# New order lists for a hand-scheduled scan kernel, and the last step of a batch sent from its own buffers

## The chip, the cores and the metric

The kernel runs on one core of a Trainium2 chip. The metric is device time in microseconds, the median of the runs; the kernel before has a median of 1783.09 us over 3 runs (1782.42 to 1785.32). The core has five engines that work side by side and wait for each other through semaphores: PE (matrix multiplies), DVE (vector), ACT (scalar functions), POOL (GpSimd) and SP, which here only issues transfers. Each engine, and each queue of transfers, works strictly in the order in which its instructions were written.

## The reference

A map of 4 batches x 128 channels x 96 x 96 is normalised in 32 groups of channels, read in four directions (rows forward and backward, columns forward and backward), and each sequence of 9216 positions goes through the same small state-space block. The four results are fused by a 1x1 convolution and added to the input.

```python
t = _grouped1x1(x, in_proj_w, in_proj_b, G)
u, gate = (t[:, :HID], t[:, HID:])
u = jax.nn.silu(u)
u = lax.conv_general_dilated(u, dw_w, ..., feature_group_count=HID)
s = _conv1x1(u, ssm_in_w)
a = DMIN + (DMAX - DMIN) * jax.nn.sigmoid(_conv1x1(u, ssm_delta_w, ssm_delta_b))
...
hst = jnp.exp(prefix) * jnp.cumsum(bb * s * jnp.exp(-prefix), axis=-1)
u = u + _conv1x1(cc * hst + ssm_d[None, :, None] * s, ssm_out_w)
u = _grouped1x1(u * jax.nn.sigmoid(gate), mix_w, mix_b, G)
return _conv1x1(u, out_proj_w, out_proj_b)
```

## The kernel before, in words

**Tiling.** A batch is worked on in two phases, columns ("V") and then rows ("H"). A phase has 6 steps of 4 units, so a phase has 24 units, a batch 48, and the kernel 192 (`NPAIR`). A unit is a pair: 384 positions of the forward sequence and 384 of the backward one, treated together. In the second half of a phase the backward sequence passes the places that the forward one has passed before, so the in-projection and the gates of the first half are kept in DRAM and read again instead of being computed twice.

**Operations.** Each unit goes through about sixty named operations. Those that the text speaks of:

- `F0` to `F3`: in-projection on PE, four matmuls of 32 rows x 32 columns each, from the tile `x_in`; `SIL0` to `SIL3`: silu on ACT (L650), which empties the PSUM bank into the tile `sil`. `zero_ends` (L657) clears the first column at the start of a sequence.
- `C0`, `C1`, `L`: depthwise convolution of the first 128 channels on PE (tiles `band`, `less`), emptied by `UC` on ACT (L751). `T0` (ACT, L786) and `T1` to `T4` (DVE, L788): the five taps for the other 128 channels.
- `P0a` to `P1b`: projections to the scan's operands on PE (`u,main`), emptied by `TM`, `SC`, `CT` on ACT. `DEC` (L826) and `BS` (L829) on POOL prepare the scan, `SCAN0` and `SCAN1` on DVE (L846) run it for a whole step, `CH`, `ADD`, `CP` on POOL (L852, L856, L859) take its result on.
- `S` and `G`: output of the scan and gates on PE (L869, L875); `GAT` on DVE (L922); `W`: mix, output projection and fusion as one product on PE (`u,w_fin`).
- `YS0`, `YS1`: ACT copies the result of a unit's two sequences from PSUM into tiles `ys` (two buffers for sequence 0, one for sequence 1; L933, L935). `ACC0`, `ACC1` (L975): POOL adds them to `acc`, the sum of the whole map, which starts as the input. `send` (L939) writes finished parts of `acc` to the output, `load_next` (L949) fills them with the next batch's input for the next sums.

**What sets the order.** Everything from the first in-projection on is recorded under a manual schedule: the order in the code is the order on each engine. Units 0 to 7 run by the list `START` (L153), the last 6 and what is still open by `END` (L116), and in between one slot per unit by one of four lists in `PLAN` (L65) that are repeated: "front" where the in-projection runs, "gate" where gates are computed, "both" and "none". `LAGS` (L87) says how many slots behind the slot's own number an operation's unit lies, `BANKS` which of the 8 PSUM banks it asks for, `MOVES` in which order the slot's transfers are issued, all on SP. In the lists a star marks the same work on another engine (`DEC*` on DVE, `CP*` on ACT, `ACC0*` straight from PSUM on DVE).

**The opening.** Before the schedule starts, `load_x` (L394) loads batch 0 in pieces of 1 to 4 chunks of 384 columns and DVE runs one `bn_stats` (L398) on each chunk; the sums give the normalisation, which is folded into the weights `wn`, and with these the first in-projection can start. Weights (`small`, `fuse`, `main`) are loaded between the pieces.

**The batch change.** A part of `acc` is worked through three times by transfers: after its last sum `send` writes it out, after that transfer has landed `load_next` overwrites it with the next batch's input, and only after that may POOL add the next batch's first results to it. For the very last step of the kernel (L972) the sums go to the free tile `x_in` and out from there.

Of the kernel before, what the change touches and what calls it, by code (L numbers as in the profile page):

```python
# [47 lines left out]
P = 128  # L48
# [18 lines left out]
        T1 F1 F3 CP YS1 TM F2 F0 DEC P1b T2 P0b W01 AU0 SIL1 SIL3 SIL0 W00 SC BS T3 T4 SIL2 ZERO  # L67
        UND1 SCAN0 UND0 AU1 YS0 G00 C0 C1 S11 CT SS S00 ACC0 ACC1 S10 G01 SCAN1 S01 CH BN G10 E
        AFTER TH0 G11 L W10 W11 GAT0 TH1 UC P0a GAT1 ADD TH2 P1a T0 TH3
    """,  # L70
    "both": """
        YS1 T1 F2 F0 TM CP SCAN1 T2 F3 F1 C0 C1 SIL1 SIL0 P0b SIL2 T3 DEC SIL3 ZERO P1b L S11
        S10 T4 CT CH G10 SS G00 UC ADD TH2 W01 UND1 E AFTER W00 SC G01 ACC1 BN S01 YS0 ACC0 S00
        UND0 G11 AU1 TH0 GAT1 AU0 W10 W11 TH1 SCAN0 BS GAT0 P0a P1a T0 TH3
    """,
    "gate": """
        P0b YS1 CP AU1 P1b ACC1 T1 TM T2 AU0 UND1 C1 DEC CT C0 SC W00 L T3 SS T4 UND0 W01 BS S11
        E AFTER SCAN1 S10 G00 CH UC YS0 S00 G01 G11 TH0 BN S01 ACC0 G10 SCAN0 TH1 GAT1 W11 W10
        ADD P1a T0 P0a TH3 GAT0 TH2
    """,  # L80
    "none": """
        C0 T1 C1 TH1 P0b L W00 CP T2 P1b YS1 W01 TH0 TM ACC1 TH3 UND0 CH UC S01 E AFTER UND1 SC
        DEC T3 YS0 S00 G10 G11 AU0 S10 S11 T4 SCAN1 CT G01 BS BN G00 ADD SCAN0 GAT1 ACC0 AU1 TH2
        T0 P0a W10 SS W11 P1a GAT0
# [12 lines left out]
        "TB": 3, "CB": 7, "SS1": 6, "PA": 6, "W0b": 0, "W1b": 6, "Fb3": 7, "Gb0": 3, "Gb3": 4  # L97
    },
    "both": {
        "SS1": 6, "PB": 6, "W0b": 2, "Fb2": 7, "Fb3": 7, "Gb3": 4  # L100
    },
    "gate": {
        "SS0": 2, "SS1": 3, "PB": 3, "W0b": 1, "W1b": 3, "Fb1": 7, "Fb2": 7, "Fb3": 7, "Gb1": 2,
        "Gb3": 3
    },
    "none": {
        "SS0": 4, "SS1": 6, "PB": 6, "W1b": 7
# [9 lines left out]
    YS1:-14=3 C1:-6 TM:-7=7 CP*:-12 C0:-6=0 W00:-13 T1:-6=2 W01:-13=2 T2:-6 P0b:-7=0 P1b:-7=3  # L117
    UND1:-12 E:-6 UND0:-12=1 ACC1:-14 T3:-6 S10:-12=4 T4:-6 S00:-12 YS0:-13=0 SC:-7 DEC:-7
    S11:-12=5 S01:-12=0 GAT0:-12=2 T0:-5=5 W11:-13 ACC0:-13 T1:-5=2 W10:-13=0 CH:-11 BS:-7
    ACC1*:-13 ADD:-11 C0:-5=6 CT:-7=6 GAT1:-12=6 P0a:-6=7 C1:-5 CH:-10 UND0:-11=0 CP:-11 T2:-5=7  # L120
    P1a:-6=1 TM:-6=4 L:-5 W00:-12 CH:-9 T3:-5 P0b:-6=7 ADD:-9 W01:-12=5 S00:-11=6 UC:-5
    UND1:-11=4 DEC:-6 T4:-5=6 S01:-11=7 ACC0*:-12 S11:-11 T0:-4=5 GAT0:-11 S10:-11=4 SS:-8
    P0a:-5 P1a:-5=1 W11:-12=7 P1b:-6=4 W10:-12=7 TM:-5=1 T1:-4=3 P1b:-5=6 SC:-6 CT:-6=6 YS1:-12
    ADD:-10 T2:-4 P0b:-5=2 T3:-4=2 C0:-4 W00:-11=6 SC:-5=5 GAT1:-11=6 DEC:-5 BS:-6 T4:-4=6
# [22 lines left out]
    W11:-3=7 CP:-1 W10:-3=2 UND1:-1 GAT1:-2=2 W00:-2=6 S11:-1=3 ACC1*:-3 S01:-1 S00:-1=3 S10:-1  # L147
    YS1:-6 YS1:-4=0 W01:-2=5 YS0:-3=1 YS1:-3 W10:-2 W11:-2 GAT0:-1=2 W00:-1 ACC0*:-2 W01:-1=0
    YS1:-2=6 GAT1:-1=4 ACC1*:-2 YS0:-2=7 W11:-1=0 ACC0*:-1 W10:-1=0 YS1:-5=6 YS0:-1 ACC1*:-1
    YS1:-1=0  # L150
"""
TAIL = 6
START = """  # L153
# [1134 lines left out]
```

## Time and profile before

| | |
|---|---|
| median of 3 runs | 1783.09 us (1782.42 to 1785.32) |
| profiled execution | 1780.91 us, of which its span is 1779.2 us |
| mean granted PE clock | 0.991 |
| PE / DVE / ACT / POOL busy | 1751.6 / 1519.3 / 1484.4 / 1400.3 us |
| HBM read / written | 222.96 / 151.18 MB |

The profile is of one execution. "Busy" is the time in which an engine has at least one instruction under way. PE's instructions overlap (four matmuls on separate quarters of the array run at once, and each matmul is two records), so its pace is read from the distance of the starts, not from the length of one record. The name of a tile stands without its number in the profile (`u,main` are the projections, `u,w_fin` the result products, `sil,band` the convolution, `x_in,wn` the in-projection and, in L875, the gates).

### The profile page before, as it was taken

To read this page: it belongs to the slowest core of one execution; us is meant where nothing else is said; L and a number is where in the kernel's file an instruction comes from. 1 tells how busy PE (TensorE), PEld (TensorE's weight loads), DVE (VectorE), ACT (ScalarE), POOL (GpSimd) and SP (SyncE) were. 2 spreads that over 40 slices of the span, in tenths; PEclk is the share of its full clock that TensorE was granted. 3 is DMA by queue.
4 is the path that set the end of the run, shared out by engine and by line. 5 is a ranking of instruction groups with operands and counts; after the bars stand their busy time and mean duration, and the time that the engine had idled before them with its cause. 6 is when DMAs were issued, how large, how long until landed. Compare 5 with 4: busy or idle time off the path is not lost.

```text
span 1779.2 us, 54578 instructions
## 1 busy us (share of the span) xinstructions
PE 1751.6 (98%) x22584; PEld 641.0 (36%) x22584; DVE 1519.3 (85%) x1550; ACT 1484.4 (83%) x2571; POOL 1400.3 (79%) x1493
## 2 busy tenths in 40 slices
PE   6999999999999999999999999999999999999998
PEld 3333333333333333333333333333333333333333
DVE  4898988888788988988788888898888878888898
ACT  4888888888888888888887888888888888888875
POOL 4488888778778888788777888878778788887776
PEclk7999999999999999999999999999999999999999
DMA  6767676665987678564798657755588755655654
GB/s 211 193 217 241 186 224 179 200 218 165 296 261 240 207 207 241 181 203 166 217 288 263 229 188 226 222 178 196 165 268 264 249 197 185 207 162 187 227 179 158
DMA packets 183143, 377.69 MB, mean 212 GB/s; under 512 B 16752, under 2 KB 146928, under 8 KB 182896
## 3 DMA queue, kind: packets, MB, share of 16 engines
q1 hardware_dynamic: 182752, 374.16, 67.1%
q8 instruction: 178, 2.92, 0.7%
q14 instruction: 69, 0.57, 0.1%
q10 hardware_dynamic: 144, 0.04, 0.0%
HBM read 222.96 MB, written 151.18 MB: 210 GB/s over the span
## 4 chain that ended last, share of the span: by engine, by line
PE 90%; DMA 3%; ACT 3%; issue 1%; SPq 1%; DVE 1%; POOL 1%; POOLq 0%; ACTq 0%; DVEq 0%
PE psum L246 76%; PE psum L869 9%; PE psum L875 4%; DMA out<-acc 1%; ACT gate L881 1%; DMA acc<-in_xr 1%; DMA main<-in_main 1%; POOL acc L975 1%; ACT psum L865 0%; SPq L716 0%; SPq L396 0%; DVE u L769 0%; ACT u L751 0%; DVE u L922 0%; POOL t L852 0%
## 5 line engine op out<-in xcount | busy, mean ns | idle before, releaser
L788 DVE SCALAR_TENSOR_TENSOR psum<-sil,small,psum 128x768 f32<-128x768 f32 x576 | 588.3, 1021 | 52.3 <-ACT psum L786 33.8
L246 PE MATMUL psum<-u,w_fin 128*32 128x384 f32 x6144 | 580.4, 490 | 1.9 <-DVE u L769 0.6
L246 PE MATMUL psum<-u,main 128*32 128x384 f32 x6144 | 563.7, 489 | 2.1 <-ACT gate L881 0.8
L975 POOL TENSOR_TENSOR acc<-ys,acc 128x384 f32<-128x384 f32 x368 | 427.5, 1170 | 154.6 <-ACT ys L935 77.6
L922 DVE SCALAR_TENSOR_TENSOR u<-gate,psum 128x768 f32<-128x768 f32 x376 | 345.9, 950 | 98.1 <-PE psum L869 67.9
L246 PEld LDWEIGHTS psum<-u,main 128*32 128x32 f32 x6144 | 186.9, 110 | 327.6 <-issue 218.2
L246 PEld LDWEIGHTS psum<-u,w_fin 128*32 128x32 f32 x6144 | 175.4, 109 | 344.3 <-issue 234.8
L865 ACT COPY psum<-u 128x768 f32<-128x768 f32 x352 | 278.0, 801 | 24.7 <-DVE u L769 8.4
L246 PE MATMUL psum<-sil,band 128*32 128x384 f32 x3072 | 287.0, 488 | 4.5 <-ACT ys L935 2.5
L852 POOL TENSOR_TENSOR t<-t,t 64x384 f32<-64x384 f32 x192 | 235.0, 1225 | 65.4 <-DVE t L846 29.2
L869 PE MATMUL psum<-t,main 32*128 32x384 f32 x1536 | 258.1, 531 | 2.6 <-ACT psum L865 2.3
L856 POOL TENSOR_TENSOR t<-t,t 64x384 f32<-64x384 f32 x192 | 237.3, 1236 | 7.6
L881 ACT ACTIVATE gate<-psum,bnorm 128x384 f32<-128x384 f32 x384 | 211.5, 576 | 35.5 <-PE psum L869 14.9
L829 POOL TENSOR_TENSOR t<-t,tm 64x384 f32<-64x384 f32 x192 | 194.8, 1014 | 52.4 <-ACT t L812 35.0
L826 POOL TENSOR_SCALAR t<-tm 64x384 f32<-64x384 f32 x189 | 181.1, 958 | 66.6 <-issue 31.0
L650 ACT ACTIVATE sil<-psum,bnorm 128x385 f32<-128x385 f32 x384 | 200.1, 580 | 27.5 <-PE psum L246 26.6
L788 DVE SCALAR_TENSOR_TENSOR u<-sil,small,psum 128x768 f32<-128x768 f32 x192 | 194.6, 1013 | 18.6 <-DVE psum L788 0.5
L786 ACT ACTIVATE psum<-sil,small 128x768 f32<-128x768 f32 x192 | 173.8, 905 | 35.1 <-DVE u L922 27.4
L875 PE MATMUL psum<-x_in,wn 32*128 32x384 f32 x768 | 186.5, 516 | 0.2
L804 ACT ACTIVATE tm<-psum,small 128x384 f32<-128x384 f32 x192 | 112.4, 585 | 58.0 <-PE psum L246 55.9
L935 ACT COPY ys<-psum 128x384 f32<-128x384 f32 x281 | 134.5, 479 | 24.7 <-POOL acc L975 13.6
L246 PEld LDWEIGHTS psum<-sil,band 128*32 128x32 f32 x3072 | 97.4, 110 | 155.8 <-issue 104.3
(84 smaller groups left out, 1446.6 us busy)
## 6 DMA issues: line engine op xcount, KB each, us to landing
sil<-sil SPq DMA_DIRECT2D x128, 770.0 KB, 7.2
kept<-gate SPq DMA_DIRECT2D x80, 768.0 KB, 4.3
gate<-kept SPq DMA_DIRECT2D x76, 768.0 KB, 5.9
edge<-edge SPq DMA_DIRECT2D x96, 384.0 KB, 5.8
x_in<-in_xs SPq DMA_DIRECT2D x192, 96.2 KB, 3.7
edge<-sil SPq DMA_DIRECT2D x96, 192.5 KB, 3.5
out<-acc SPq DMA_DIRECT2D x44, 384.0 KB, 3.4
acc<-in_xr SPq DMA_DIRECT2D x38, 384.0 KB, 8.4
```

What stands on the lines that cost most here:

```text
L246: nc.tensor.matmul(o[r, : rhs.shape[-1]], lhsT, rhs, start=start, stop=stop, skip_group_check=True)
L650: nc.scalar.activation(sils[step][:, s, j, g, :], bank(frm)[:, : N + 1], AF.Silu, bias=bn[:, 1:2] if j else bn[:, 4 + g : 5 + g],)
L788: nc.vector.scalar_tensor_tensor(u_of(n)[:, :, 1, :] if k == K - 1 else part, src, w_tap[:, k : k + 1], part, ALU.mult, ALU.add,)
L829: nc.gpsimd.tensor_mul(scan_of(n)[0:64, pair_of(n)["p"], :], tbs[n][0:64, :], tms[n][0:64, :])
L852: nc.gpsimd.tensor_mul(ta[0:64, p, :], tbs[n][64:P, :], ta[64:P, p, :])
L856: nc.gpsimd.tensor_add(z, scans[n // R][0:64, pair_of(n)["p"], :], z)
L865: nc.scalar.copy(two(to), us[n][:, s])
L869: nc.tensor.matmul(bank(to)[:, :N], w_so[r, bass.ts(j, P)], tbs[n][r, :], start=not seeded(n), stop=True, skip_group_check=True)
L875: nc.tensor.matmul(bank(to)[:, :N], stats[pair_of(n)["b"]][0][r, s, :], x_in[s][r, q, off : off + N], start=True, stop=True)
L881: nc.scalar.activation(gates[n % 2][:, s, j, :], bank(frm)[:, :N], AF.Tanh, bias=bn[:, 2 + j : 3 + j], scale=0.5,)
L922: nc.vector.scalar_tensor_tensor(v, g, 1.0, two(frm), ALU.add, ALU.mult)
L975: nc.gpsimd.tensor_add(to, y, part)
```

## The change

**Lists.** `PLAN`, `LAGS`, `BANKS`, `START` and `END` are replaced by new ones with the same operations for the same units. `T1` now is recorded one slot ahead of its unit (lag -1, before 0), `ADD`, `TH2` and `TH3` one slot later (lag 6, before 5). `END` has `BS*` and `CH*` once each (the same product on DVE), no `DEC*` (before 3), and `CP*` 7 times (before 5).

**Opening.** The pieces of batch 0 are 1, 1, 2, 2 chunks and then nine of 2, with `fuse` after the first four. The first columns of `sil` are cleared on POOL in two parts, each after the two silus that it needs, before on DVE after all four. The next step's `x_in` is loaded for each of the four in-projections as soon as its own four units are through, before for all four together unit by unit. The layout of `sil` has its two middle dimensions exchanged; sizes and numbers of transfers of it stay.

**Batch change.** The sums of the last four units of a batch no longer go back into `acc`: sequence 0's goes in place into `ys`, sequence 1's into a tile `fin` of two buffers (the space of the tile `xs`), and each is written out from there (192 KB instead of 384 KB, twice as many). `acc` is loaded anew as soon as POOL's sums of these parts have read it. `load_next` is called once more at the end of the two slots 7 and 8 of a batch.

```diff
 PLAN = {
     "front": """
-        T1 F1 F3 CP YS1 TM F2 F0 DEC P1b T2 P0b W01 AU0 SIL1 SIL3 SIL0 W00 SC BS T3 T4 SIL2 ZERO
...
+        F1 G01 YS1 F3 T2 TM T3 F2 F0 TH1 ADD P1b AU0 SIL1 SIL3 DEC P0b SIL0 C0 CP AU1 TH2 SIL2
...
-    load_x([(0, 1), (1, 2), (3, 3)])
+    load_x([(0, 1), (1, 1), (2, 2), (4, 2)])
     w_small = load(small, "small")
-    load_x([(6, 4)])
     w_out_fuse = load(fuse, "fuse", pp, nc.sync)
-    load_x([(10, 4)])
-    load_x([(14, 4), (18, 4), (22, 2)])
+    load_x([(c, 2) for c in range(6, NSC, 2)])
...
     def send(s):
+        for frm, to in sends[s]:
+            nc.sync.dma_start(frm, to)
+        sends[s].clear()
...
-        y = yss.pop((n, s)) if frm is None else bank(frm)[:, :N]
+        result = y = yss.pop((n, s)) if frm is None else bank(frm)[:, :N]
...
-        final = n >= NPAIR - R
-        to = x_in[s][:, p, :N].rearrange("p (h m) -> p h m", m=M) if final else part
+        final = n % (2 * NP) >= 2 * NP - R
+        to = part
+        if final:
+            here = x_in[s][:, p, :N]
+            if n < NPAIR - R:
+                if un["b"] not in fins:
+                    fins[un["b"]] = wk.tile([P, 2, SC], F32, tag="xs", bufs=1, name=f"fin_{n}")
+                here = fins[un["b"]][:, n % 2, :] if s else result
+            to = here.rearrange("p (h m) -> p h m", m=M)
...
-            nc.sync.dma_start(out[un["b"], :, bass.ts(R * st + p, N)], x_in[s][:, p, :N])
+            sends[s].append((out[un["b"], :, bass.ts(R * st + p, N)], here))
+            if n >= NPAIR - TAIL:
+                send(s)
+        if final and un["b"] + 1 < B:
+            added[s] += 1
+            if added[s] % R == 0:
+                reload.extend((now[0] - 2, un["b"] + 1, bass.ts(2 * st + e, LN * WW // 2)) for e in range(2))
...
+        if t % (2 * NP) in (7, 8):
+            load_next()
```

How the instructions move, at three places. First SP's queue at the first batch change. `out_0` is the result, `in_xr` the input, `acc_69` the sum; `ys_46` and `ys_47` are the results of sequence 0 of the last two units of batch 0, `fin_44` the tile for sequence 1. Before:

```order
L941 DMA out_0<-acc_69 128x768 x2
L896 DMA kept0_0_254<-gate0_252 128x1536
L952 DMA acc_69<-in_xr 128x768 x2
L716 DMA edge0_2_292<-sil_14_5426 32x4x385 x4
L941 DMA out_0<-acc_69 128x768 x2
L384 DMA x_in0_70<-in_xs 64x385
L384 DMA x_in1_71<-in_xs 64x385
L896 DMA kept0_1_255<-gate1_253 128x1536
L952 DMA acc_69<-in_xr 128x768 x2
```

And of the change, from the result of unit 46 on:

```order
L940 DMA out_0<-ys_46_0_5572 128x384
L759 DMA edge_54_5604<-edge0_1_296 128x2x384
L940 DMA out_0<-fin_44_5345 128x384 x2
L383 DMA x_in0_70<-in_xs 64x385
L383 DMA x_in1_71<-in_xs 64x385
L940 DMA out_0<-ys_47_0_5678 128x384
L893 DMA kept0_0_259<-gate0_257 128x1536
L954 DMA acc_69<-in_xr 128x768 x4
L713 DMA edge0_2_297<-sil_14_5418 32x4x385 x4
L940 DMA out_0<-fin_44_5345 128x384
```

The last loads of `acc` no longer follow the transfer that sends the same part out; they stand ahead of the edge transfers and read nothing that is still on its way out.

Second PE in the opening, after the first sixteen in-projections. `x_in,wn` is the in-projection of the next step's units, `sil,band` and `sil,less` the convolution, `u,main` the projections (`u_0` is unit 0, `u_1` unit 1). Before:

```order
L246 MATMUL psum_72<-sil_0_369,band_140 32x384 x4
L246 MATMUL psum_72<-x_in0_70,wn_0_325 32x385 x8
L246 MATMUL psum_72<-x_in1_71,wn_0_325 32x385 x4
L246 MATMUL psum_72<-sil_0_369,band_140 32x384 x4
L246 MATMUL psum_72<-sil_0_369,less_141 32x384 x8
L246 MATMUL psum_72<-x_in0_70,wn_0_325 32x385 x4
L246 MATMUL psum_72<-x_in1_71,wn_0_325 32x385 x12
L246 MATMUL psum_72<-u_0_516,main_126 32x384 x8
L246 MATMUL psum_72<-sil_0_369,band_140 32x384 x4
L246 MATMUL psum_72<-u_0_516,main_126 32x384 x8
L246 MATMUL psum_72<-sil_0_369,band_140 32x384 x4
```

And of the change:

```order
L245 MATMUL psum_72<-sil_0_374,band_145 32x384 x4
L245 MATMUL psum_72<-sil_0_374,less_146 32x384 x8
L245 MATMUL psum_72<-x_in1_71,wn_0_330 32x385 x4
L245 MATMUL psum_72<-x_in0_70,wn_0_330 32x385 x8
L245 MATMUL psum_72<-u_0_493,main_131 32x384 x4
L245 MATMUL psum_72<-x_in0_70,wn_0_330 32x385 x4
L245 MATMUL psum_72<-x_in1_71,wn_0_330 32x385 x4
L245 MATMUL psum_72<-u_0_493,main_131 32x384 x4
L245 MATMUL psum_72<-sil_0_374,band_145 32x384 x4
L245 MATMUL psum_72<-x_in1_71,wn_0_330 32x385 x8
L245 MATMUL psum_72<-u_0_493,main_131 32x384 x4
```

The first convolution (`band x4`) and the first in-projection of the next step (`x_in0 x4`) stand just ahead of this piece. In the new order in-projections stand between the projections; before, six groups on all 128 rows (`u`, `band`, `u`, `band`) follow each other without one.

Third POOL in a "gate" slot, where the scan's operands of unit 33 are made. `t0_8` are these operands for step 8 (`TENSOR_SCALAR` is `DEC`, the product with `tm_33` is `BS`), `t0_7<-t1_29` and `t1_29<-t0_7` are `CH` and `ADD` of unit 29, the copies are `CP`, `acc_69<-ys` the sums. Before:

```order
L859 COPY t1_28_3136<-t1_28_3136 64x384
L975 TENSOR_TENSOR acc_69<-ys_26_1_3614,acc_69 128x16x24
L826 TENSOR_SCALAR t0_8_3543<-tm_33_3623 64x384
L829 TENSOR_TENSOR t0_8_3543<-t1_33_3632,tm_33_3623 64x384
L852 TENSOR_TENSOR t0_7_3114<-t1_29_3246,t0_7_3114 64x384
L975 TENSOR_TENSOR acc_69<-ys_27_0_3666,acc_69 128x16x24
L856 TENSOR_TENSOR t1_29_3246<-t0_7_3114,t1_29_3246 64x384
```

And of the change:

```order
L856 COPY t1_28_3133<-t1_28_3133 64x384
L823 TENSOR_SCALAR t0_8_3553<-tm_33_3630 64x384
L826 TENSOR_TENSOR t0_8_3553<-t1_33_3633,tm_33_3630 64x384
L985 TENSOR_TENSOR acc_69<-ys_27_0_3662,acc_69 128x16x24
L849 TENSOR_TENSOR t0_7_3120<-t1_29_3249,t0_7_3120 64x384
L985 TENSOR_TENSOR acc_69<-ys_26_1_3617,acc_69 128x16x24
L853 TENSOR_TENSOR t1_29_3249<-t0_7_3120,t1_29_3249 64x384
```

The sum of sequence 1 (`ys_26_1`), whose tile has a single buffer, moved from the start of the slot to behind `DEC`, `BS`, the sum of the next unit's sequence 0 and `CH`.

More of the change, by code (lines that the diff above doesn't have):

```diff
@@ L116 @@
 END = """
[L117 to L122, printed above, removed]
@@ L660, in zero_ends @@
         if step % NS == 0:
-            engine = nc.gpsimd if step else nc.vector
             for s in range(2):
-                engine.memset(sil[64 * s : 64 * s + 64, s, 0, g, 0:1], 0.0)
-            if g < 2:
-                engine.memset(sil[:, :, 1, g, 0:1], 0.0)
+                if 0 in parts:
+                    nc.gpsimd.memset(sil[64 * s : 64 * s + 64, 0, s, g, 0:1], 0.0)
+            if g < 2 and 1 in parts:
+                nc.gpsimd.memset(sil[:, 1, :, g, 0:1], 0.0)
     def load_silu(step, gs):
@@ L724, in blocks @@
     def blocks(step):
-        return [sils[step][:, s if fresh(step) else 1 - s, 0] for s in range(2)]
+        return [sils[step][:, 0, s if fresh(step) else 1 - s] for s in range(2)]
     def conv(n, s, to):
```

190 lines of the change are left out of this document (108 added, 82 removed), and 10 rows, old and new, of the table LAGS.

## Prediction

> **What bounds the kernel now.** I read the page's first two parts, then windows over the whole span, then the chain and the timeline at the three places where the windows show PE idle.
>
> ```profile
> span 1779.2 us, 54578 instructions
> PE 1751.6 (98%) x22584; PEld 641.0 (36%) x22584; DVE 1519.3 (85%) x1550; ACT 1484.4 (83%) x2571; POOL 1400.3 (79%) x1493
> PE   6999999999999999999999999999999999999998
> PEclk7999999999999999999999999999999999999999
> ```
>
> PE has work under way for 98% of the span; all its idle time together is 27.6 us, 1.6%. The first digits of both lists (a slice is 44.5 us) say where most of it lies: in the opening, at a low clock. In the middle the windows give PE no idle time at all, while DVE, ACT and POOL each have some to spare:
>
> ```profile
> 205.00:214.00 9.00, 9.00 (x136) 3.15 (x132) 7.98 (x8) 7.86 (x14) 7.48 (x8) 1.00 0.86 246
> 214.00:223.00 9.00, 9.00 (x132) 3.12 (x124) 8.79 (x10) 7.97 (x15) 7.57 (x11) 1.00 0.81 245
> ```
>
> (Columns: length, then busy time and count of PE, weight loads, DVE, ACT, POOL; clock; DMA share; GB/s.) So the kernel runs at PE's pace, and a new order is worth only what it takes from PE's idle time, from the slow clock, or from PE's own work. I counted that work in both orders, four matmuls on the array's quarters as one group: 2413 groups before, 2412 now, with 748 and 750 changes of the matmul's shape. It is the same. Three places are left.
>
> **The opening.** DVE's statistics wait for their pieces, then run without a gap to 18.91:
>
> ```profile
>   DVE bn L398: 3.4, 4
> 12.27 6.64 DVE L398 BATCH_NORM_STATS2 bn<-acc 128x6 f32<-128x384 f32 x14 [1.20 <-DMA acc<-in_xr]
> 18.93 0.27 DVE L431 TENSOR_SCALAR main<-main 128x64 f32<-128x64 f32 x1
> 19.04 0.80 DVE L296 BATCH_NORM_AGGREGATE mv<-bn 128x2 f32<-128x144 f32 x1
> DMA to landing us min/median/max: 2.7/9.1/11.5
> L396 SPq DMA_DIRECT2D acc<-in_xr x8: 393/432/1370, 0.8 to 5.5; - x8
> ```
>
> The last piece, issued at 5.5, lands at 17.0 at the latest (11.5 later), so from then on DVE, not the transfer, is late. Smaller pieces take away waits early in the row: the end comes down to the last landing plus two records of 0.474 (6.64 / 14), 17.95, and the scaling of `main` now stands behind the aggregate: 0.9 us sooner. Five more issues of 0.43 on SP lie under transfers already queued. Bounds: nothing, and 1.1.
>
> Then sixteen silus must pass ACT before the first convolution:
>
> ```profile
> 27.64 3.91 ACT L650 ACTIVATE sil<-psum,bnorm 128x385 f32<-128x385 f32 x8 [1.18 <-PE psum L246]
> 32.51 2.47 ACT L650 ACTIVATE sil<-psum,bnorm 128x385 f32<-128x385 f32 x5 [0.96 <-PE psum L246]
> 34.77 1.66 PE L246 MATMUL psum<-sil,band 128*32 128x384 f32 x8 [1.48 <-DVE sil L663]
> 46.01 2.79 PE L246 MATMUL psum<-u,main 128*32 128x384 f32 x16
> 49.55 1.46 PE L246 MATMUL psum<-u,main 128*32 128x384 f32 x16
> ```
>
> Two groups (16 records) take 2.79 us at 46 and 1.46 at 49.55; without the last record's overlap a group is about 1.3 us at half clock and 0.65 at full. The silus could follow at 0.49 (3.91 / 8); ACT lost 1.18 + 0.96 waiting for in-projections. Walked through by hand with these durations, the new order keeps some of those waits (`F2:0` and `F2:1` come only in the third and fourth set of four) and ends its silus near 33.4 instead of 34.98, of which 0.9 is the earlier start; the first convolution starts near 33.7, 1.1 sooner. From there both are bound by PE at half clock:
>
> ```profile
> 30.00:40.00 10.00, 8.41 (x72) 1.98 (x56) 4.56 (x14) 5.32 (x11) 0.00 (x0) 0.50 0.46 127
> 40.00:50.00 10.00, 10.00 (x92) 2.42 (x92) 3.68 (x4) 5.14 (x9) 0.00 (x0) 0.54 0.86 218
> 46.00:48.00 2.00, 2.00 (x20) 0.61 (x20) 1.75 (x2) 1.62 (x4) 0.00 (x0) 0.50 1.12 218
> 48.00:50.00 2.00, 2.00 (x24) 0.70 (x20) 1.93 (x3) 0.00 (x0) 0.00 (x0) 0.69 1.03 250
> ```
>
> The clock steps up at 49.2 (0.69 over 48 to 50), although PE was busy without a gap from 38 on. What is new from 46.0 on are groups on all 128 rows, one after another. The new list reaches such a run later, since it puts in-projections between them: ten sets of 1.3 to 1.4 us after 33.7, near 47.4. By then it has done three groups that the old order still had to do at 46.0: 3.9 us of half-speed work for 1.4 us more time, 1.2 us ahead at full speed, the 0.9 of the start included. If the clock steps up at 49.2 again, the opening gains 1.2; if it needs 3.2 us of such groups as before (46.0 to 49.2), it comes at 50.6, and the extra 1.4 us at half rate cost 0.7. I take -0.6, and as bounds a step one 3.2 us stretch earlier (-2.9) or two later (+2.2).
>
> [...]
>
> **The batch changes.** The chain at the first:
>
> ```profile
> 523.57 5.59 DMA out<-acc
> 529.22 5.00 DMA acc<-in_xr
> 535.71 2.38 POOL acc L975 x2
> 538.12 0.48 ACT ys L935
> ACT ys L935 <- POOL acc L975: 2.0, 1, 2.0
> ACT ys L935 <- POOL acc L975: 2.4, 1, 2.4
> ACT ys L935 <- POOL acc L975: 1.8, 1, 1.8
> ```
>
> The sum goes out (5.59 us), only then the next input comes in (5.00), POOL adds, and ACT, which stood 2.0 us before a full `ys`, goes on; the three waits are those of the three changes. Behind ACT's copy stand the tanh and the copies that PE's next groups need. PE's loss is its idle time there:
>
> ```profile
> 520.00:540.00 20.00, 19.25 (x240) 6.97 (x240) 16.94 (x16) 15.67 (x28) 13.00 (x13) 1.00 1.01 323
> 540.00:560.00 20.00, 19.51 (x228) 7.60 (x220) 17.27 (x19) 17.93 (x32) 18.89 (x17) 1.00 0.77 236
> 950.00:970.00 20.00, 20.00 (x268) 7.06 (x268) 17.13 (x16) 16.45 (x29) 11.63 (x11) 1.00 0.98 324
> 970.00:990.00 20.00, 18.32 (x208) 7.33 (x204) 17.77 (x20) 15.96 (x29) 19.07 (x17) 1.00 0.79 251
> 1390.00:1410.00 20.00, 19.07 (x219) 7.25 (x215) 18.90 (x18) 16.09 (x29) 14.27 (x12) 1.00 1.00 341
> 1410.00:1430.00 20.00, 19.90 (x241) 7.52 (x239) 14.81 (x16) 17.55 (x32) 18.84 (x19) 1.00 0.47 157
> ```
>
> 0.75 + 0.49, 1.68, 0.93 + 0.10: 3.95 us in all. The change takes the 5.59 out of the chain; ACT waited at most 2.4, so the whole wait goes. New on SP are four more issues per change and the edge transfers behind four loads in a row (4 x 0.43, about 2 us later, with a slot of about 9 us, 1779.2 / 192, as cover), and `ys` stays taken until its transfer has landed: 5.6 us against two slots. I take -3.2, bounds -3.95 and 0. What is late next there is POOL itself, 18.9 busy of 20 after the change.
>
> **The end.** `DEC*` on DVE is on the chain:
>
> ```profile
> 1744.78 2.83 DVE t L826 x2
> L826 DVE TENSOR_SCALAR t<-tm x3: 503/1489/1494, 1744.8 to 1750.0; 64x384 f32<-64x384 f32 x3
> 1740.00:1760.00 20.00, 18.96 (x225) 6.67 (x220) 18.87 (x20) 14.78 (x25) 16.50 (x15) 1.00 0.42 146
> ```
>
> Two of the three take 1.49 us, one 0.50: they run beside POOL, which reads the same tiles' rows at that time. They hold up the gating behind them on a DVE that is 94% busy, and PE idles 1.04 us. The new list leaves all three to POOL and gives DVE one `BS*` and one `CH*`, not seen in this trace; the nearest row is this one, 0.5 to 1.5, and I take the upper end, 3.0 for 3.5 removed. What counts is that nothing of it is known to stand before the gating: -1.0, bounds -1.04 and +1.5 (one of the two in that place).
>
> [...]
>
> **The lists of the middle.** DVE's order there is the same but for a few swaps; POOL's and ACT's differ. PE has no idle time to give: 0, bounds -3 and +3, from the waits that the trace shows on ACT before POOL (13.6 in all, 6.2 of it at the batch changes).
>
> ```profile
> ACT ys L935 <- POOL acc L975: 13.6, 20, 2.4
> ```
>
> **Sum.** -0.6 - 3.2 - 1.0 + 0 = -4.8 us. The profiled execution took 1780.91, 1.71 more than its span; it becomes 1776.1. The median of the runs is 2.18 higher, so I forecast 1778.3 (-0.27%).
>
> **Rivals.** *The slow clock lasts longer*: the interleaved in-projections keep it two stretches longer, +2.2 instead of -0.6: 1781. For it speaks that the run of full groups starts later; against, that the threshold is unknown. 0.08.
> *The reload isn't sooner*: SP is held by the transfers ahead of `acc`'s loads, which wait for POOL and DVE, and the 3.2 stay: 1781.5. Against it: the loads need only the sums, and these were through before the old transfer out began at 523.57. 0.06.
> *Slower, through `ys1`*:
>
> ```profile
> L829 POOL TENSOR_TENSOR t<-t,tm 64x384 f32<-64x384 f32 x192 | 194.8, 1014 | 52.4 <-ACT t L812 35.0 <-ACT tm L804 7.9 <-DMA gate<-kept 1.1
> L975 POOL TENSOR_TENSOR acc<-ys,acc 128x384 f32<-128x384 f32 x368 | 427.5, 1170 | 154.6 <-ACT ys L935 77.6 <-ACT ys L933 63.2 <-issue 2.7
> ```
>
> The sum of sequence 1 now stands behind four instructions (`DEC`, `BS`, a sum, `CH`) of 1.0 to 1.2 us, 4.4 us, so its single buffer comes free in the second half of the slot, with some 3 us of 9 left before the next copy. From the point where POOL runs over 3 us late, ACT waits in every such slot, and everything behind its copy with it. At 0.68 us each (13.6 / 20), half of it passed on to PE, in the 48 slots that follow the 48 steps' scans: +16, 1794. Against it, POOL itself idles 154.6 us before its sums, so it is rarely late. 0.16.
> *Faster*: the clock steps up early and the lists take the remaining small waits: -2.9 - 3.95 - 1.04 - 3 = -10.9, 1772. 0.22.
>
> **Chances.** My forecast 0.48 (three quarters of it below 1779.5). Faster by over 0.2% (3.6 us, about what a measurement of this kernel can tell from no change): 0.36 + 0.22 = 0.58. Within: 0.12 + 0.08 + 0.06 = 0.26. Slower: 0.16. The range reaches from below the faster case (1768) into the slower one (1788).
>
> **What would show it.** Right: ACT's wait before POOL's sums gone at all three changes, and PE without idle time in those windows; the first convolution near 33.7 and the clock's step between 47 and 53; no 1.49 us `DEC` on DVE at the end. Wrong: idle time of PE in the middle windows, or ACT waiting for POOL in many slots.

## The result, and the profile after

The changed kernel has a median of 1796.49 us (1796.02 to 1798.37, 4 runs); the kernel before, on the same chip, 1782.76 (1779.49 to 1785.32, 4 runs). The ratio is 1.0079, with a 95% interval of 1.0066 to 1.0092: **slower by 14 us**, where 1778.3, faster, had been forecast. The profiled execution took 1796.02 us, 1.7 more than its span.

First lines of the page of the changed kernel, then windows over the second batch change and the tail (columns as in the prediction: after the stretch and its length, PE, weight loads, DVE, ACT, POOL, then the granted clock, DMA share, GB/s):

```profile
span 1794.3 us, 54421 instructions
PE 1756.6 (98%) x22584; PEld 632.2 (35%) x22584; DVE 1506.8 (84%) x1539; ACT 1466.6 (82%) x2573; POOL 1403.9 (78%) x1502
```

```profile
940.00:960.00 20.00, 18.21 (x232) 6.06 (x232) 15.58 (x16) 13.55 (x26) 11.12 (x12) 0.91 0.51 167
1720.00:1740.00 20.00, 16.48 (x172) 5.35 (x168) 14.85 (x15) 11.45 (x19) 14.46 (x13) 0.86 0.66 233
```

PE now idles 37.7 us (span less busy), 10 more than before, and two things are new: at 940 to 960 and at 1720 to 1740 it idles 1.8 and 3.5 us, and there the clock is at half again for a while (0.91 and 0.86 of full over 20 us). These are the rows of waits that stand out; the first is the one on ACT's copies, which had 13.6 us, 20 times, before:

```profile
ACT ys L932 <- POOL acc L985: 53.1, 92, 1.6
PE psum L245 <- DVE u L766: 2.3, 1, 2.3
DVE u L766 <- DMA edge<-edge: 2.2, 1, 2.2
POOL acc L985 <- DVE acc L987: 3.9, 1, 3.9
DVE t L843 <- POOL t L826: 4.2, 1, 4.2
PE psum L245 <- DVE u L785: 2.1, 1, 2.1
PE psum L866 <- ACT psum L862: 1.5, 2, 0.9
```

(The first is of the whole span, the next two of 930 to 945 us, the others of 1700 to 1745: engine and line that waited, what for, total, times, longest.) They name three suspects: the buffers of `ys`, the transfer of the edge (`edge<-edge`, a load that DVE's tap in L766 needs), and a sum in the tail.

To see how much lies where, I took from each trace the starts of the 6144 result matmuls (`u,w_fin`, 32 a unit) and compared their distances with those of before. "Opening" is the start of the first, "middle" the units 0 to 44, 52 to 92, 100 to 140 and 148 to 176, "changes" the three stretches of 8 units between them, "end" from unit 176 to the last result matmul. Differences against before's trace in us. "Half clock" counts pieces of 3.41 us at half clock in the opening, at the changes and in the end; before has 9, 0 and 0, and the last section says what they are. The ratios are against before on the same chip. T stands for the tail's sum moved, E for the edge first, S for the sum `ACC1` early; all are told below.

| kernel | median us | ratio (95%) | opening | middle | changes | end | half clock |
|---|---|---|---|---|---|---|---|
| the change | 1796.5 | 1.0079 (1.0066 to 1.0092) | -3.9 | +8.3 | +5.2 | +5.3 | 7, 1, 2 |
| tail_acc: T | 1790.2 | 1.0037 (1.0022 to 1.0051) | -2.9 | +9.5 | +10.4 | -1.5 | 7, 3, 0 |
| edge_first: E | 1796.8 | 1.0067 (1.0052 to 1.0081) | -3.8 | +10.2 | +1.4 | +4.4 | 5, 0, 2 |
| acc1_only: S | 1789.8 | 1.0032 (1.0019 to 1.0044) | -4.2 | +2.3 | +4.8 | +4.1 | 6, 2, 1 |
| combo: T, E | 1789.1 | 1.0026 (1.0017 to 1.0035) | -0.5 | +10.6 | +0.8 | -1.5 | 9, 0, 0 |
| acc1_tail: T, S | 1782.6 | 0.9991 (0.9978 to 1.0004) | -4.2 | +2.8 | +0.1 | -1.5 | 5, 1, 0 |
| **combo_acc1: T, E, S** | **1777.0** | **0.9960 (0.9948 to 0.9972)** | -4.5 | +4.6 | -2.8 | -1.5 | 7, 0, 0 |
| ys_ring: T, E, ring | 1784.0 | 0.9998 (0.9985 to 1.0011) | -0.2 | +6.5 | +1.5 | -1.4 | 9, 0, 0 |
| ring_acc1: T, E, S, ring | 1777.5 | 0.9961 (0.9948 to 0.9973) | -1.7 | +3.3 | -2.0 | -1.3 | 6, 0, 0 |
| acc1_gate: T, E, half of S | 1786.0 | 1.0012 (1.0004 to 1.0021) | -2.8 | +5.7 | +0.3 | -1.5 | 7, 0, 0 |
| batch_old: old batch change | 1806.2 | 1.0127 (1.0112 to 1.0143) | -3.5 | +10.1 | +16.2 | +5.2 | 5, 5, 2 |
| acc1_batch_old: T, E, S, old batch change | 1782.3 | 0.9988 (0.9975 to 1.0000) | -4.0 | +4.8 | +1.9 | -1.5 | 7, 1, 0 |
| lists_old: old lists, new code | 1793.7 | 1.0053 (1.0040 to 1.0066) | +0.1 | -0.4 | +10.8 | +0.4 | 8, 3, 0 |
| before_open: before, new opening | 1780.7 | 0.9979 (0.9969 to 0.9988) | -3.9 | +1.3 | +2.6 | +0.4 | 5, 0, 0 |
| best1: before_open, new end | 1781.4 | 0.9987 (0.9978 to 0.9996) | -3.1 | +3.3 | +0.6 | -0.1 | 7, 0, 0 |

The first row adds up to 15.0 of the 15.1 us by which the span grew; the rest lies behind the last result matmul. Each row's parts are of one execution, in `tail_acc` the slowest of its five (1796.5), and they scatter. The changes run by the same code in the first two rows and measure +5.2 and +10.4; two of the pieces at half clock, 1.7 us of work each, are 3.4 of the difference. The middle of `before_open` and `best1` is that of before and measures +1.3 and +3.3. So parts that differ by less than about 3 us decide nothing here, and the ratios, which rest on 4 to 12 runs, come first.

### The profile page after: what moved, and what is told of

Its sections match the earlier page's. It is cut to its first block, busy times and chain, and to the rows that moved or that the text cites. A ratio compares the mean times of both kernels' runs of the same rounds, so it can differ in the third digit from the quotient of the medians.

```text
span 1794.3 us, 54421 instructions
## 1 busy us (share of the span) xinstructions
PE 1756.6 (98%) x22584; PEld 632.2 (35%) x22584; DVE 1506.8 (84%) x1539; ACT 1466.6 (82%) x2573; POOL 1403.9 (78%) x1502
## 4 chain that ended last, share of the span: by engine, by line
PE 78%; POOL 7%; ACT 5%; DMA 4%; DVE 3%; issue 2%; SPq 1%; DVEq 0%; POOLq 0%; ACTq 0%
PE psum L245 67%; PE psum L866 5%; PE psum L872 5%; POOL acc L985 4%; POOL t L849 2%; DMA edge<-edge 1%; ACT psum L862 1%; ACT gate L878 1%; DMA acc<-in_xr 1%; DVE psum L785 1%; DVE u L919 1%; DVE t L843 1%; ACT sil L647 1%; DMA edge<-sil 1%; ACT ys L930 0%
## 5 line engine op out<-in xcount | busy, mean ns | idle before, releaser
L245 PE MATMUL psum<-u,w_fin 128*32 128x384 f32 x6144 | 593.8, 491 | 6.9 <-DVE u L766 4.5
L985 POOL TENSOR_TENSOR acc<-ys,acc 128x384 f32<-128x384 f32 x344 | 411.2, 1204 | 186.8 <-ACT ys L932 93.4
L245 PE MATMUL psum<-sil,band 128*32 128x384 f32 x3072 | 302.4, 490 | 10.2 <-ACT gate L878 9.1
L866 PE MATMUL psum<-t,main 32*128 32x384 f32 x1536 | 264.0, 532 | 1.5 <-ACT psum L862 1.5
L849 POOL TENSOR_TENSOR t<-t,t 64x384 f32<-64x384 f32 x191 | 234.3, 1227 | 29.4 <-DVE t L843 15.3
L878 ACT ACTIVATE gate<-psum,bnorm 128x384 f32<-128x384 f32 x384 | 221.9, 578 | 38.4 <-PE psum L866 17.7
L826 POOL TENSOR_TENSOR t<-t,tm 64x384 f32<-64x384 f32 x191 | 198.6, 1040 | 52.6 <-ACT t L809 26.7
L853 POOL TENSOR_TENSOR t<-t,t 64x384 f32<-64x384 f32 x192 | 233.1, 1214 | 6.3
L647 ACT ACTIVATE sil<-psum,bnorm 128x385 f32<-128x385 f32 x384 | 194.4, 583 | 28.6 <-PE psum L245 28.0
L932 ACT COPY ys<-psum 128x384 f32<-128x384 f32 x281 | 134.5, 479 | 70.5 <-POOL acc L985 53.1
L245 PEld LDWEIGHTS psum<-sil,band 128*32 128x32 f32 x3072 | 92.5, 109 | 174.6 <-issue 92.7
```

The lines of the kernel that those rows point to most:

```text
L245: nc.tensor.matmul(o[r, : rhs.shape[-1]], lhsT, rhs, start=start, stop=stop, skip_group_check=True)
L647: nc.scalar.activation(sils[step][:, j, s, g, :], bank(frm)[:, : N + 1], AF.Silu, bias=bn[:, 1:2] if j else bn[:, 4 + g : 5 + g],)
L826: engine.tensor_mul(scan_of(n)[0:64, pair_of(n)["p"], :], tbs[n][0:64, :], tms[n][0:64, :])
L849: engine.tensor_mul(ta[0:64, p, :], tbs[n][64:P, :], ta[64:P, p, :])
L853: engine.tensor_add(z, scans[n // R][0:64, pair_of(n)["p"], :], z)
L866: nc.tensor.matmul(bank(to)[:, :N], w_so[r, bass.ts(j, P)], tbs[n][r, :], start=not seeded(n), stop=True, skip_group_check=True)
```

## Experiments

**Two halves apart: batch_old, lists_old.** The theory was that the new waits lie at the batch changes and in the tail (A), the rival that the buffer `ys1` costs nearly everything (B). `batch_old` takes back the code of the batch change:

```diff
-        final = n % (2 * NP) >= 2 * NP - R
...
+        final = n >= NPAIR - R
+        to = x_in[s][:, p, :N].rearrange("p (h m) -> p h m", m=M) if final else part
...
-        if t % (2 * NP) in (7, 8):
-            load_next()
```

> The changed kernel with the old handling of the batch change: sums of a batch's last four units go back into acc, send writes acc out, the reload waits for that. Lists, opening and end stay new. Theory A (the new waits are at the three batch changes and in the tail): the trace of the change shows the edge transfer issued 4.7 us later than before and landing 2.2 us too late at the second change, where PE stands 2.3 us and then runs 3.4 us at half clock; without that, 5 us less, 1791.5 (1788.5 to 1793.5). Theory B (the single buffer ys1 in the slots of the middle costs nearly all of the 14 us): the old batch change gives nothing back, or loses the 3.2 us that were forecast for it: 1796 to 1800.

1806.2, slower than the change by 10 us: against both theories. Around the second change of this kernel:

```profile
968.12 4.25 DMA out<-acc
ACT ys L932 <- POOL acc L978: 6.5, 2, 5.9
PE psum L245 <- ACT gate L878: 5.3, 1, 5.3
```

The old chain is back (the transfer out, the sum on POOL, ACT's copy), and with the new lists ACT waits 5.9 us for it, where before it waited 2.4. Five pieces at half clock follow at the three changes, 8.5 of the 16.2 us there. `lists_old` is the other half, all tables as before and the rest as in the change:

```diff
-        F1 G01 YS1 F3 T2 TM T3 F2 F0 TH1 ADD P1b AU0 SIL1 ...
+        T1 F1 F3 CP YS1 TM F2 F0 DEC P1b T2 P0b W01 AU0 ...
```

> All tables (slot lists, lags, banks, opening list, end list) as before; the code of the batch change, the pieces of the first load and the opening's clears as in the change. Theory A: the batch change alone costs 2 to 6 us on the old lists too, since its sends stand ahead of the edge transfers there as well: 1785 to 1789. Theory B: with the old place of the sum of sequence 1 the waits of ACT for POOL are gone, and the batch change brings its forecast 3.2 us: 1779 to 1781. ACT's waits at ys before POOL fall from 53 us to under 16 by both.

1793.7, above even the range of theory A, nearly all of it at the changes (+10.8). At the first:

```profile
522.93 5.37 DMA acc<-in_xr
POOL acc L986 <- DMA acc<-in_xr: 5.9, 1, 5.9
DVE t L844 <- POOL t L827: 3.4, 1, 3.4
PE psum L246 <- ACT gate L879: 3.1, 1, 3.1
```

The reload is issued sooner (522.93, before 529.22), but the first sum that needs it also stands sooner in POOL's queue: POOL stands 5.9 us before it, `BS` behind it holds the scan for 3.4, and PE loses 3.1. So each half costs time without the other, and neither alone is the cause. Theory A as stated fell too; what stayed are its places.

**The tail: tail_acc (T).** In the changed kernel's chain a sum on DVE (`ACC0*` of unit 180, L987) releases one on POOL (`ACC1` of unit 179, L985), since both add to the same part of `acc`:

```profile
1720.30 0.63 DVE acc L987
...
1720.99 1.69 POOL acc L985
...
1730.50 1.01 POOL t L826
...
1731.53 2.58 DVE t L843
```

POOL stood 3.9 us before the sum; `DEC` (1722.78) and `BS` (1730.50) behind it came late for the scan at 1731.5, and PE behind that.

```diff
-    ... CT:-6 ACC0*:-12 SC:-6=3 L:-5=0 ACC1:-13
+    ... CT:-6 ACC1:-13 ACC0*:-12 SC:-6=3 L:-5=0
```

> One entry of the end list moved: the sum ACC1 of unit 179 (on POOL) is recorded ahead of ACC0* of unit 180 (on DVE), which adds to the same part of acc, instead of behind it. In the trace of the change POOL stood 3.9 us before this sum, waiting for DVE's; its later DEC and BS then held DVE's scan for 4.2 us, PE stood 2.1 + 1.5 us and ran 6.8 us at half clock. Theory A: 5.5 us less, 1791 (1789 to 1793), with no half clock in the tail. Theory B, or that another wait of the tail comes up in the same place: 1795.5 to 1797.

1790.2, 6 us less than the change (7.5 by the ratios), as theory A said. PE's window there, of this kernel:

```profile
1720.00:1740.00 20.00, 20.00 (x248) 7.16 (x240) 17.97 (x20) 15.22 (x26) 17.30 (x16) 1.00 0.68 232
```

No idle time, full clock; the end went from +5.3 to -1.5. One entry of the list cost 6.8 us. With the early sum in place the same edit is worth as much: 7.3 us by the ratios of `acc1_only` and `acc1_tail`.

**The order on SP: edge_first (E).** SP's queue in the changed kernel at the second change (start, duration):

```profile
930.80 0.57 SPq L940 DMA_DIRECT2D out<-ys  x1
931.42 1.18 SPq L759 DMA_DIRECT2D edge<-edge  x1
```

Before, with DVE's tap that needs this load; then from the chain of the changed kernel, and its tap:

```profile
926.76 0.63 SPq L762 DMA_DIRECT2D edge<-edge  x1
936.65 1.01 DVE L769 SCALAR_TENSOR_TENSOR u<-edge,small,psum 128x768 f32<-128x768 f32 x1 [0.82 <-PE psum L875]
```

```profile
931.42 9.18 DMA edge<-edge
940.72 1.01 DVE L766 SCALAR_TENSOR_TENSOR u<-edge,small,psum 128x768 f32<-128x768 f32 x1 [2.16 <-DMA edge<-edge]
```

The load is issued 4.7 us later than before, behind more transfers, among them a send that waited at most 0.5 us for POOL's sum. By the result matmuls the whole kernel is 3.0 us behind at this place (unit 92), so against the work the load is about 1.7 us later. Its 9.2 us are no new cost: before, the same load took 9.8 us and landed at 936.6, 0.1 us before the tap began. DVE had been free for the tap 0.8 us sooner (the profile puts that wait down to PE), so nothing was to spare.

```diff
-    "front": "LS XG KG XC LF KS SEND0 LE SEND1 LK",
-    "both": "LS XC LF KS LE SEND1 XG SEND0 LK KG",
+    "front": "LE LS XG KG XC LF KS SEND0 SEND1 LK",
+    "both": "LE LS XC LF KS SEND1 XG SEND0 LK KG",
```

> The order of a slot's transfers on SP alone changed, in the slots of kind front and both: the load of the edge (LE) first, the sends of results last. Theory A: the edge no longer stands behind sends that wait for POOL's sums; if it lands in time, 2 to 4 us less, 1792.5 to 1794.5, and no half clock at the second batch change. If the edge's late landing comes from the 9.2 us that its transfer takes beside the others, and not from its place on SP: 1796 to 1798. Theory B: 1796.5.

By the median nothing is decided: 1796.8 lies in the range of the case that the place on SP does not matter, and the ratio is 0.0012 lower, with intervals that overlap. Its trace, of the fastest of its five runs, has the edge's load at 928.9, no half clock at this change, and the changes at +1.4 instead of +5.2. `combo` puts T and E together:

> The changed kernel with both edits that were tried apart: ACC1 of unit 179 ahead of ACC0* of unit 180 in the end list, and in the slots front and both the edge's load first and the sends last. From the distance of the same matmuls in the traces the tail lost 5.3 us against before and the batch changes 5.2; the first edit took 6.8 from the tail, the second about 4.8 from the batch changes. If the two add up: 9 us under the change, 0.2% over before, 1787 (1784.5 to 1789). If the batch changes come out by chance in each run and the second edit did nothing: 1790 to 1792.

1789.1, a little over the range for two edits that add up and just under that for an E that does nothing; the opening of its profiled execution came out 3.3 us later than that of the change. What E does is seen in DVE's waits for the edge, here of the change, `tail_acc`, `combo` and `combo_acc1` over the whole span (before: 1.9, 2 times):

```profile
DVE u L766 <- DMA edge<-edge: 9.0, 8, 2.2
DVE u L766 <- DMA edge<-edge: 14.0, 9, 2.8
DVE u L766 <- DMA edge<-edge: 3.0, 2, 1.5
DVE u L766 <- DMA edge<-edge: 0.5, 1, 0.5
```

That it counts in the time is shown further down, by `acc1_tail`.

**The early sum: combo_acc1, acc1_only (S).** `ACC1` moved in all four lists, here "gate":

```diff
-        P0b T2 P1b TH3 YS1 ADD TH2 C1 C0 T3 AU0 TM CP SC W01 ...
-        P0a BN P1a GAT0 ACC1 SS T1
+        P0b T2 P1b TH3 YS1 ADD TH2 C1 C0 T3 AU0 TM CP ACC1 SC W01 ...
+        P0a BN P1a GAT0 SS T1
```

> The kernel with both edits, and in all four slot lists the sum ACC1 moved from the end of the slot to right behind CP, so that POOL empties the single buffer ys1 early, as before the change. Theory A (ACT's copy waits for that sum, ACT's tanh stands behind the copy, and PE waits for the tanh's bank; the middle lost 8.1 us in units 0 to 40, 52 to 92 and 100 to 140): ACT's waits at ys for POOL fall from 53 us to under 20, and 3 to 6 us go: 0.2 to 0.35% under the kernel with both edits. Rival: ACT's waits at ys are off the path, and the middle lost by the order on PE itself: within 1 us of it. Rival on the other side: the sum ahead of DEC and BS delays the scan: 2 us slower.

1777.0, **12 us less than `combo`, twice the most that was expected, and faster than the kernel before** (ratio 0.9960). ACT's wait for POOL's sums, 52.0 us in `combo`, has left the list of waits, and PE has no idle time behind the second change:

```profile
span 1775.2 us, 54644 instructions
PE 1751.6 (99%) x22584; PEld 635.0 (36%) x22584; DVE 1498.1 (84%) x1539; ACT 1463.9 (82%) x2573; POOL 1438.2 (81%) x1502
```

```profile
940.00:960.00 20.00, 20.00 (x280) 6.79 (x280) 16.18 (x18) 16.04 (x31) 12.37 (x14) 1.00 0.86 280
```

> The change with ACC1 moved to right behind CP in the four slot lists and nothing else; tail and order of SP's transfers as in the change. With tail and transfers mended this move took 12 us (1789.1 to 1777.0). If its share adds to the others: 10 us under the change, 1786 (1784 to 1788.5), about 0.15% over before, with the half clock in the tail still there. If it only pays once the other two are mended: 1790 or more.

1789.8: by the ratio 8.4 us less, between the two cases. The middle gives the same 6.0 us as on `combo` (8.3 to 2.3, and 10.6 to 4.6); at the changes, which differ from run to run, it gives 0.4 here and 3.6 there. By the ratios S is worth 8.4 us alone, 8.2 on `tail_acc` and 11.8 on `combo`, and E 2.0 us without S (`tail_acc` to `combo`) and 5.5 with it: each may bring its full worth only with the other, but with intervals of some 2 us to either side of a ratio the 8.4 and the 11.8 are not told apart for certain.

**Buffer or place in the queue: ys_ring, ring_acc1.** The same space, the sum still late, but a copy no longer waits for the sum just ahead:

```diff
-        ... tag=f"ys{s}", bufs=2 - s, name=f"ys_{n}_{s}")
+        ... tag="ys", bufs=3, name=f"ys_{n}_{s}")
```

> The kernel with both edits (tail, edge first); ACC1 stays at the end of the slots. The three buffers of ys (two for sequence 0, one for sequence 1) become one ring of three, in the same space: a copy then waits for the sum three copies back and not for that of the unit just ahead. The order on every engine stays. If the single buffer is the cause: ACT's waits at ys for POOL fall from 52 us to under 15 and 7 to 12 us go: 1777 to 1782. If it is the place of ACC1 in POOL's order that holds up others: 1787 to 1790.

1784.0: between the two again, 5 us. ACT's wait before `ys` for POOL's sums is gone entirely, but another has come, before its copy into `t` (L809), for POOL's `ADD` (L853); `combo` does not list this one:

```profile
ACT t L809 <- POOL t L853: 13.8, 31, 0.5
```

POOL's lateness reaches ACT through the next buffer. How much of the 7 us that are left goes this way was not measured.

> The fastest kernel (tail, edge first, ACC1 right behind CP: 0.9960 of before) with the one ring of three buffers for ys as well. If what the late ACC1 cost was the single buffer, and the ring gave only part back because the sum's lateness then reached ACT through another buffer (the trace of the ring shows ACT before its copy into t waiting for POOL's ADD, 8 times), the ring adds nothing here: 0.994 to 0.998 of before. If single buffer and place in POOL's order are two causes that add up: 4 us faster still, 0.992 to 0.994.

0.9961 against 0.9960: with the sum early the ring adds nothing. So it is one cause, the late place of the sum, and the single buffer was one of its ways to ACT.

`acc1_gate` moves the sum as `combo_acc1` does, but in the lists "gate" and "none" alone:

> The kernel with both edits (tail, edge first: 1.0026 of before) with ACC1 moved to right behind CP in the lists gate and none alone (12 of 24 slots of a phase); in front and both it stays at the end. By the traces the move took 9.6 us after the opening, of which the stretches that hold the gates' slots (units 8 to 40 and 100 to 108 among them) show the waits of PE for ACT's gate. If these slots carry the cost: 8 to 12 us under the kernel with both edits, 0.996 to 0.998. If all slots carry it alike: half, 0.999 to 1.000. If the slots of the batch change (front and both) carry it: 1.001 to 1.003.

1.0012 against 1.0026: by the ratios only 2.5 of the 11.8 us, the third case. By the traces the lists "gate" and "none" give 4.9 of the 6.0 us of the middle and 0.6 of the 3.6 at the changes, which would leave the batch changes to "front" and "both". The two measures fit only loosely; how the shares divide stays open.

**The batch change on lists that bear it: acc1_batch_old, acc1_tail.** The edits are those shown above: T, E, S and the old code of the batch change; and T and S without E.

> The fastest kernel so far (tail, edge first, ACC1 early: 1777.0) with the old handling of the batch change (sums back into acc, sent from there, the reload behind that transfer). If the new handling brings what was forecast once its own waits are gone: 3 us slower, 1780 (1779 to 1782). If the new lists cannot bear the old handling, as on the change as it stood (9.7 us): 1785 to 1788.

1782.3, between the two ranges: the old handling costs 5 us (0.9988 against 0.9960, and the intervals do not touch), 4.7 by the traces (+1.9 against -2.8). The new handling brings its time.

> The fastest kernel so far without the edit of SP's order: the edge's load stands behind the sends of results again. If that order costs what the traces of the change show at the batch changes (up to 4.8 us): 1779 to 1782. If the early sums of POOL already let the sends go in time: 1776.5 to 1778.5.

1782.6, 5.5 us over the kernel with E, just above the first range (the intervals do not touch): the order on SP does count, and DVE's wait for the edge is 7.2 us here against 0.5 there. Its chain at the second change, where DVE waits 2.9 us:

```profile
926.55 9.19 DMA edge<-edge
...
935.86 1.03 DVE u L766
```

**The opening alone, and with the end list: before_open, best1.** The kernel before with the new `START` (with `TH2:2 TH3:2 ADD:2` added and `T1:8` taken away, as the old lags ask), pieces, clears and loads of `x_in`; `best1` also with the mended `END` (banks renamed, `T1:-6` added, `ADD:-12` taken away).

```diff
-    load_x([(0, 1), (1, 2), (3, 3)])
+    load_x([(0, 1), (1, 1), (2, 2), (4, 2)])
...
-            after(every(ss, [n]), lambda n=n: zero_ends(n))
+            after(every(ss[1::2], [n]), lambda n=n: zero_ends(n, (1,)))
+            after(every(ss[::2], [n]), lambda n=n: zero_ends(n, (0,)))
```

> The kernel before with the opening of the change alone: its list for units 0 to 7 (with the few operations added or taken away that the old lags ask for), its pieces of the first load, its clears and loads of x_in. By the traces the first result product of unit 0 starts at 84.4 us of the span with the new opening and at 88.1 with the old one. If that holds: 3.7 us under before, 1780 (1778.5 to 1781.5). If the clock steps up as late as with the old list (49.2 instead of 41.5): within 1 us of before.

1780.7, ratio 0.9979: 3.7 us, as expected.

> The kernel before with the opening of the change and its end list with the one entry moved; slot lists, lags, banks and batch change as before. By the traces the end list as mended is 1.5 us shorter from unit 176 on than the old one: 1.5 us under the kernel with the new opening alone, 5 us under before, 1778.5 (1776.5 to 1780.5), faster than both. If the end list owes its time to the new lags: no faster than with the new opening alone.

1781.4, above its range: the end list brings nothing on the old lists (end -0.1 in the trace), so the 1.5 us that it is shorter in the other kernels belong to it together with the lists ahead of it.

## Why the prediction was wrong, point by point

**The opening (-0.6 forecast, -3.9 measured): right in sign, but three steps failed.** The first is the start, which did not move as forecast: the five more issues did not lie under transfers already queued. The nine issues behind `fuse` took 7.2 us, the last piece left at 10.05 and landed at 18.35, and the first in-projection starts at 23.87, 0.7 later than before (23.15) and not 0.9 sooner. The first convolution starts at 33.11 (forecast 33.7), right. The second is the clock's: it steps up at 41.3, not near 47.4 or later:

```profile
10.05 8.30 DMA acc<-in_xr
23.87 7.34 PE psum L245 x110
...
33.11 15.07 PE psum L245 x137
```

```profile
17.00:18.00 1.00, 1.00 (x8) 1.00 (x7) 0.94 (x2) 0.00 (x0) 0.91 (x4) 0.73 1.12 277
41.00:42.00 1.00, 1.00 (x20) 0.15 (x8) 0.00 (x0) 1.00 (x2) 0.00 (x0) 0.83 0.62 154
```

(Three pieces of the chain, then 1 us windows at both ends of the half clock. Before, three pieces of the chain:)

```profile
34.62 3.32 DMA x_in<-in_xs
37.99 12.05 PE psum L246 x97
58.36 12.07 PE psum L246 x162
```

The list reaches no run of full groups before 41.3, so such a run is not what the clock waits for. The third is "from there both are bound by PE at half clock". From 33.11 to 87.3 the chain of the change holds nothing but PE. Before, it ran through a load of `x_in` (34.62 to 37.94), which I had passed over, and from 50.4 to 58.3 through ACT and DVE, which prepare the tap behind which PE goes on at 58.36. `lists_old`, with the old list, goes on at 58.16 although its clock was up at 44.7, and gains nothing (+0.1); it also waits 4.1 us for the same load, so it is the list, not the new code of these loads, that took both off the chain.

With the new list the clock then does count, and it differs from run to run. Where the half clock lasted to 48.9 and 49.8 (`combo`, `ys_ring`, 9 pieces as before) the opening gains 0.5 and 0.2 us, about what was forecast; where it ended between 36.3 and 42.0 it gains 2.8 to 4.5 (1.7 in `ring_acc1`, with one more piece at 63.7). So part of the -3.9 is this run's luck, though 12 of the 14 traces with the new list ended early, and `before_open` keeps 3.7 us over ten runs. Why the clock mostly steps up sooner stays open. One sum was off too: with the stretches of 3.2 us that it names, the forecast's bounds come to -2.8 and +2.0, not -2.9 and +2.2.

**The batch changes (-3.2 forecast, +5.2 measured): the mechanism was right, the cover failed.** I let the edge's load stand about 2 us later "with a slot of about 9 us as cover". Against the work it was 1.7 us later, as said, but the slot was no cover: the transfer itself took 9.8 us there before and 9.2 after, and DVE waited 2.2 us for it. With edge and sum mended the stretch measures -2.8, and the new handling by itself is worth about 5 us (`acc1_batch_old`).

**The end (-1.0 forecast, +5.3 measured): the step "nothing of it is known to stand before the gating" failed.** I priced `BS*` and `CH*` and looked no further. They cost 0.92 and 0.87 us, below my 1.5:

```profile
1720.95 0.87 DVE L849 TENSOR_TENSOR t<-t,t 64x384 f32<-64x384 f32 x1
1720.99 1.69 POOL L985 TENSOR_TENSOR acc<-ys,acc 128x384 f32<-128x384 f32 x1 [3.93 <-DVE acc L987]
1767.26 0.92 DVE L826 TENSOR_TENSOR t<-t,tm 64x384 f32<-64x384 f32 x1
```

The loss came from two sums to one part of `acc` on two engines: POOL stood 3.9 us before its own until DVE's was through. Without it the list is 1.5 us shorter than before's, near the -1.0 that was forecast, but `best1` shows that it is so only with the new lists ahead of it. In the second row the sum on POOL, beside `CH*` on DVE, took 1.69 us, against a mean of 1.20 for these sums; whether `CH*` lengthened it was not measured.

**The middle (0 forecast, +8.3 measured): the rival of `ys1` was the right one.** Its mechanism, the sum behind `DEC`, `BS`, a sum and `CH`, is what the runs show, with 6.0 us in the middle and 3.6 more at the changes (`combo` to `combo_acc1`, 0.8 to -2.8): 9.6 by the traces, 11.8 by the ratios (8.4 with S alone), against a price of 16. I gave it 0.16 because POOL idles 154.6 us before its sums and so seemed rarely late. That step failed: the idle time was no reserve. After the change it is larger (186.8 us) while ACT waits 92 times for the same sums, 53.1 us in all, where the price had 48 waits more.

```profile
L985 POOL TENSOR_TENSOR acc<-ys,acc 128x384 f32<-128x384 f32 x344 | 411.2, 1204 | 186.8 <-ACT ys L932 93.4
```

Here two engines waited for each other in turn, and both show idle time. What remains of the middle in the fastest kernel, +4.6, was not followed; `best1`, with the old middle, has +3.3.

**What the parts add to.** -3.9 + 8.3 + 5.2 + 5.3 = 14.9 (15.0 before rounding) of the 15.1 us of span. Of the four terms two came out with the other sign, the batch changes and the end, and the middle, put at nothing, was the largest. In all three I costed the operations that were moved, and not what waits behind them. Once the three waits are mended the same lists are 7.1 us faster than before (0.9960), more than the 4.8 that were forecast.

## What to carry to other kernels

When an order changes, ask of every instruction that now stands later who fills or empties its buffer next, and of every instruction that waits, what stands behind it on the same queue; idle time of the waiting engine is no evidence that it has time to spare (POOL idled 154.6 us before its sums, and their later place still made ACT wait 53.1). Two adds to one place on two engines are a wait between their queues (3.9 us on POOL in the tail): record them in the order in which the engines reach them. Undoing a whole block can mislead: without the new batch change the kernel was slower still (`batch_old`), although that part brings 5 us once the waits are gone. So undo a suspected wait rather than a block of code.

## What the runs showed of the hardware

**In these traces half clock came in whole pieces of 3.41 us.** In the opening it lasts from 18.50 to 49.22 before (30.7 us, 9 pieces), from 17.46 to 41.34 in the changed kernel (23.9, 7 pieces; rows above: 0.73 means that 0.54 of this us ran at half), and in `edge_first` from 20.64 to 37.72 (17.1, 5 pieces). Before, then `edge_first`:

```profile
18.00:19.00 1.00, 1.00 (x9) 1.00 (x9) 0.97 (x3) 0.00 (x0) 1.00 (x4) 0.75 1.05 202
49.00:50.00 1.00, 1.00 (x16) 0.37 (x12) 0.96 (x2) 0.00 (x0) 0.00 (x0) 0.89 1.09 277
```

```profile
20.00:21.00 1.00, 0.14 (x8) 0.17 (x8) 0.92 (x2) 0.00 (x0) 1.00 (x4) 0.82 1.08 205
37.00:38.00 1.00, 1.00 (x9) 0.20 (x8) 0.96 (x2) 0.00 (x0) 0.00 (x0) 0.64 0.93 194
```

The 14 traces with the new opening list hold 5, 6, 7 and 9 pieces in it, so one list can end its slow stretch at quite different times. A piece at half clock (0.50 in the windows inside it) does 1.7 us less work, but that shows in the time only while PE alone is the limit: with 5 pieces the opening came out no shorter than with 7, and in all five such traces the chain then runs through a load of `x_in` (7.3 to 8.7 us, from 53.0 to 54.1 on), and PE stands for 0.4 to 1.6 us between 40 and 80, in the changed kernel not at all. What lifts the clock stays unexplained: 11 us of busy PE before did not, nor 16 us in `combo` (32.8 to 48.9), and the prediction's estimate from a run of full groups had no ground.

**The half clock came back behind short stalls.** The changed kernel's PE stood 2.3 us at the second change and then ran at half clock from 942.46 to 945.88 (one piece); in the tail it stood 1.5 us in two waits and 2.1 in a third, all within 6 us, and ran at half from 1734.36 to 1741.18 (two pieces):

```profile
942.00:943.00 1.00, 1.00 (x12) 0.33 (x8) 1.00 (x2) 0.36 (x1) 1.00 (x1) 0.73 1.02 359
945.00:946.00 1.00, 1.00 (x12) 0.22 (x4) 0.96 (x2) 0.04 (x1) 0.00 (x0) 0.56 1.04 355
1734.00:1735.00 1.00, 0.00 (x0) 0.00 (x0) 0.97 (x2) 0.00 (x0) 1.00 (x2) 0.68 0.15 61
1741.00:1742.00 1.00, 1.00 (x16) 0.40 (x12) 0.00 (x0) 0.43 (x2) 0.96 (x1) 0.91 0.06 16
```

So a stall of 2.3 us cost up to 4.0, and the two pieces in the tail, 3.4 us, are half of what the late sum cost. The length of a stall alone does not decide it: `before_open` stood 2.4 us at 934.2 and kept full clock, and `lists_old` fell back at 942.4 behind a single stall of 1.2 us (0.91 over 20 us, one piece):

```profile
920.00:940.00 20.00, 17.57 (x252) 6.33 (x244) 14.94 (x15) 15.25 (x28) 13.39 (x14) 1.00 1.01 296
940.00:960.00 20.00, 18.80 (x243) 5.94 (x240) 15.67 (x16) 13.41 (x26) 14.10 (x15) 0.91 0.60 190
```
